# Moving a gate's product with x from TensorE to GpSimd (layer 0) and VectorE (layer 2) in a four-layer graph network

## The chip, the core and the metric

The kernel runs on one core of one Trainium2 chip. The metric is the device time of one execution in microseconds (us). Before the change the median of 14 runs is 3122.3 us (3103.58 to 3138.67).

In the views of the profile PE is TensorE's matmul, PEld its weight load, DVE is VectorE, ACT is ScalarE, POOL is GpSimd and SP is SyncE, which issues most transfers. L1576 is line 1576 of the kernel before. A matmul with float32 operands appears as two PE instructions.

## What is computed

There are 16 graphs (batches) of 1024 nodes with 128 features and a dense 0/1 adjacency of 1024 by 1024 each. Four layers follow each other, each of the form x = layernorm(x + gnn(x, adj)). The two layers that the change touches are attention layers with gates:

```
# layer 0
h = x @ W.T + b;  e = (h @ A) @ h.T;  e = e + e.T
att = softmax(where(adj > 0, e, -9e15), axis=1) * adj
hp  = relu(att @ h)
coeff = sigmoid(concat([x, hp]) @ gate_w.T + gate_b)          # one gate
out = coeff * x + (1 - coeff) * hp
# layer 2: the same attention with zeros for the masked, and three gates
i, f, o = [sigmoid(concat([x, hp]) @ g_w.T + g_b) for g in (ig, fg, og)]
out = o * tanh(sigmoid(i * hp + f * x))
```

So a gate is a dot product of 256 numbers for each node: 128 of them meet x and 128 meet hp. Layer 1 thins the adjacency row by row and runs three neighbourhood averages with batch norms; layer 3 is a graph convolution with two propagations through the normalized adjacency.

## The kernel before

**Layout.** A batch's x lies as s.xn, a tile of 128 partitions by 8 blocks by 128 features: node 128*i + p is in partition p, block i. Its transpose xT is 128 features by 1024 nodes, and TensorE's other operands (hT, G, hpT) have this shape too. A gate's product on TensorE therefore takes block i of xT (128 by 128) as the weights and one (layer 0, L916) or three (layer 2, L1576) columns of the gate's vector as what streams through: one matmul for each block, whose result has one or three columns.

All of this is fast_kernel. A second, general kernel in the same program runs only if flags (`bad` and others) say that the inputs are not of the form that fast_kernel is made for; here it does not run.

**Streams.** Each attention layer has three generators per batch: before (loads, transposes and products up to hT, G and hn), attention (eight tiles jt of scores, mask, softmax and the product with h), and after (gate, residual, norm; in layer 2 all of layer 3 follows in it). in_turn (L793) first runs before alone, for batch 0 in layer 0 and for batches 0 and 1 in layer 2, and then attention of batch b, after of batch b-1 and before of batch b+1 in turns, one yield each. The last batch's after has no attention beside it. In what order an engine then executes is decided by the scheduler of the language's tile layer, which reorders instructions within the engines' queues; each engine then works through its queue strictly in its order, and a wait at its head holds all behind it.

**Layer 0** (us 0 to 765). before (L888) handles eight row blocks `it` of the adjacency: ACT converts a block to bfloat16 with row sums (L897), DVE checks that it holds 0 and 1 only (L900), PE transposes it (L904), DVE writes it as 8-bit floats into the carry tile (L905). Between them stand, at it == 1, the transposes that make xT; at it == 3 hT = W0T xT and the gate's product with x (L914 to L918), which DVE copies into s.gx; at it == 5 G; at it == 7 hn. attention (L930) makes scores on PE (line L723 of a helper), adds the mask and takes the row maximum on DVE (L942), exponentiates on ACT (L946), scales a block of hn (hs, L950) and adds to acc on PE (L953). after (L956) takes relu of acc as hpT (L959), multiplies with the gate's other half (L962), adds s.gx (L964), takes a tanh, and combines: tile r of the pool `work`, one buffer, takes the part of hp (L973) and is added to xn (L974). normed (L772) then takes bn_stats and bn_aggr on DVE, the power -0.5 on POOL (ln_rstd, L744), ln_nb on DVE (L782) and eight scalings on ACT (L784). POOL issues the transfers of x1 (L977) and of the carry tile (L928). All transposes, products and gate results of layer 0 besides scores and acc share two PSUM buffers (ps_h, tag "h").

**Layers 2 and 3** (us 1890 to 3130). before (L1508) finishes layer 1's output, norms it (L1521), makes xT (L1525), hT (L1529), G (L1533) and hn (L1536). s.xT has two buffers and is kept until after. attention (L1539) is as in layer 0 with another mask. after (L1569) takes hpT (L1572), and pg (L1576, L1577): for each of eight blocks a matmul on xT that starts an accumulation and one on hpT that ends it. gt is pg plus the biases (L1579), tanh (L1580) and a scaling (L1581); the combination (L1584 to L1591) and a norm follow. Then layer 3: two elu in a row (L1607 to L1613; in a half of 512 columns, exp on ACT, L1478 or L1474, and two instructions on DVE, L1479/L1480 or L1475/L1476), scaled_parts (L1482: product with a weight, L1489, scaling zn, L1491, and a split into zhi, L1492, and zlo, L1494), propagated (L1497: 32 products with the adjacency, L1503, in two halves), an elu, and both once more; a last norm and the transfer of the result. Transposes and products again share two PSUM buffers (ps_h).

**Weights.** gw (L879 and L1185) holds each gate's vector as two columns of 128, loaded with a strided transfer. row_bcast (L689) loads a row into all partitions; column (L695) loads a vector as one column. `bad` (L675) is a tile of flags that the layer-1 code sets (L1092, L1113) and the last lines sum up (L1647).

Of the kernel before, what the change touches and what calls it, by code (L numbers as in the profile page):

```python
# [9 lines left out]
F32 = mybir.dt.float32  # L10
F16 = mybir.dt.float16
F32R = mybir.dt.float32r
BF16 = mybir.dt.bfloat16
# [4 lines left out]
OP = mybir.AluOpType  # L18
AX = mybir.AxisListType
# [3 lines left out]
P = 128  # L23
# [616 lines left out]
def fast_kernel(ctx: ExitStack, tc: tile.TileContext, t: dict, out: bass.AP, flag: bass.AP):  # L640

    nc = tc.nc
    B, N, D = t["x"].shape
    NT = N // P
# [27 lines left out]
    deg = consts.tile([P, BT], F32, name="deg")  # L672
    dinv = deg

    bad = consts.tile([P, 2, NT, B], F32, name="bad")  # L675
    past = consts.tile([P, NT - 2, B], F32, name="past")
    other = consts.tile([P, BT], F32, name="other")

# [82 lines left out]
    def products(psum, *pairs):  # L761

        for p, c, _ in halves(psum):
            for i, (W, x) in enumerate(pairs):
                nc.tensor.matmul(p, W, x[:, c], start=(i == 0), stop=(i == len(pairs) - 1))  # L765
            yield p, c

    def half_rows(v):

# [97 lines left out]
    with ExitStack() as ph:  # L867
# [8 lines left out]
        work = ph.enter_context(tc.tile_pool(name="l0_work", bufs=1))  # L876
        small = ph.enter_context(tc.tile_pool(name="l0_small", bufs=2))
        b0 = column(wts, t["L0_gnn_W_b"], "l0b")
        gw = wts.tile([P, 2], F32, name="l0gw")  # L879
        with nc.allow_non_contiguous_dma(reason="a vector of 256"):  # L880
            nc.sync.dma_start(gw, t["L0_gnn_gate_w"].rearrange("o (h d) -> d (o h)", d=P))
        gb = row_bcast(wts, t["L0_gnn_gate_b"], 1, "l0gb")
        gbh = wts.tile([P, 1], F32, name="l0gbh")
        nc.vector.tensor_scalar(gbh, gb, 0.5, None, op0=OP.mult)
# [3 lines left out]
        def before(s, b):  # L888

            s.xn = work.tile([P, NT, P], F32, name="xn", bufs=3)  # L890
            nc.sync.dma_start(s.xn, nat(t["x"][b]))
            for it in range(NT):
                c = b * NT + it
                an = work.tile([P, N], F32, name="an", bufs=2)
                nc.sync.dma_start(an, t["adj"][b][it * P:(it + 1) * P, :])
                ab = work.tile([P, N], BF16, name="ab", bufs=2)
                nc.scalar.activation(ab, an, AF.Copy, accum_out=deg[:, c:c + 1])  # L897

                chk = work.tile([P, N], FP8, name="chk")
                nc.vector.scalar_tensor_tensor(chk, an, 0.0, an, op0=OP.is_gt, op1=OP.not_equal,  # L900
                                               accum_out=other[:, c:c + 1], saturate=False)
                pt = ps_h.tile([P, NT, P], BF16, name="pt", tag="h")
                for jt in range(NT):
                    nc.tensor.transpose(pt[:, jt, :], ab[:, jt * P:(jt + 1) * P], identb)  # L904
                nc.vector.tensor_scalar(Y[b][:, :, it * P:(it + 1) * P], pt, 0.0, None, op0=OP.is_gt, saturate=False)  # L905
                if it == 1:
                    xT = work.tile([P, N], F32, name="xT")
                    for p, c, _ in turned(ps_h, s.xn):
                        nc.scalar.copy(xT[:, c], p)
                elif it == 3:  # L910
                    s.hT = work.tile([P, N], F32, name="hT", bufs=2)
                    for p, c in products(ps_h, (W0T, xT)):
                        nc.scalar.activation(s.hT[:, c], p, AF.Identity, bias=b0)
                    pz = ps_h.tile([P, NT], F32, name="pz", tag="h")  # L914
                    for i in range(NT):
                        nc.tensor.matmul(pz[:, i:i + 1], xT[:, i * P:(i + 1) * P], gw[:, 0:1], start=True, stop=True)  # L916
                    s.gx = small.tile([P, NT], F32, name="gx")
                    nc.vector.tensor_copy(s.gx, pz)  # L918
                elif it == 5:
                    s.G = work.tile([P, N], F32, name="G", bufs=2)  # L920
                    for p, c in products(ps_h, (As0, s.hT)):
                        nc.scalar.copy(s.G[:, c], p)
                elif it == 7:
                    s.hn = work.tile([P, N], F32, name="hn")
                    for p, c, _ in turned(ps_h, s.hT):
# [30 lines left out]
        def after(s, b):  # L956

            hpT = work.tile([P, N], F32, name="hpT")
            nc.scalar.activation(hpT, s.acc, AF.Relu)  # L959
            pz = ps_h.tile([P, NT], F32, name="pz", tag="h")  # L960
            for i in range(NT):
                nc.tensor.matmul(pz[:, i:i + 1], hpT[:, i * P:(i + 1) * P], gw[:, 1:2], start=True, stop=True)  # L962
# [205 lines left out]
    class Layers23:  # L1168
# [8 lines left out]
        def weights(self, ps_h):  # L1177
            wts = self.wts
            self.Wl = wts.tile([P, 3, P], F32, name="Wl")
            nc.sync.dma_start(self.Wl, nat(t["L1_gnn_Wl"]))  # L1180
            self.blcol = column(wts, t["L1_gnn_bl"], "blcol")
            self.W2T = transposed(wts, ps_h, matrix(wts, t["L2_gnn_W_w"], "l2W"), "l2WT", "h")
            self.b2 = column(wts, t["L2_gnn_W_b"], "l2b")
            self.As2 = symmetric(wts, ps_h, matrix(wts, t["L2_gnn_A"], "l2A"), "l2As", "h")
            self.gw = wts.tile([P, 2, 3], F32, name="l2gw")  # L1185
            self.gb = wts.tile([P, 3], F32, name="l2gb")
            for i, n in enumerate(("ig", "fg", "og")):
                with nc.allow_non_contiguous_dma(reason="a vector of 256"):
                    nc.sync.dma_start(self.gw[:, :, i], t[f"L2_gnn_{n}_w"].rearrange("o (h d) -> d (o h)", d=P))
                src = t[f"L2_gnn_{n}_b"]  # L1190
# [31 lines left out]
    with ExitStack() as ph:  # L1222
# [187 lines left out]
        for l in range(3):  # L1410
# [9 lines left out]
            for i in range(B + lag[l]):  # L1420
# [32 lines left out]
    with ExitStack() as ph:  # L1453
# [10 lines left out]
        def wide(name, bufs=1, dtype=F32):  # L1464
            return work.tile([P, N], dtype, name=name, bufs=bufs)
# [42 lines left out]
        def before(s, b):  # L1508
# [11 lines left out]
            yield  # L1520
            normed(small, s.xn)  # L1521
            yield
            s.xT = wide("xT", 2)
            for p, c, _ in turned(ps_h, s.xn):
                nc.scalar.copy(s.xT[:, c], p)  # L1525
            yield
            s.hT = wide("hT", 2)
            for p, c in products(ps_h, (W2T, s.xT)):
# [40 lines left out]
        def after(s, b):  # L1569
# [3 lines left out]
            pg = ps_h.tile([P, NT, 3], F32, name="pg", tag="h")  # L1573
            for i in range(NT):
                c = slice(i * P, (i + 1) * P)
                nc.tensor.matmul(pg[:, i, :], s.xT[:, c], gw[:, 0, :], start=True, stop=False)  # L1576
                nc.tensor.matmul(pg[:, i, :], hpT[:, c], gw[:, 1, :], start=False, stop=True)  # L1577
# [106 lines left out]
```

## Time and profile before

| | |
|---|---|
| median of 14 runs | 3122.3 us |
| the profiled execution's own time | 3132.34 us |
| its span, first to last instruction | 3130.6 us |
| mean granted TensorE clock in it | 0.964 |
| gate products with x, layer 0 (L916) | 256 PE instructions, 30.0 us busy, mean 247 ns |
| gate products with hp, layer 0 (L962) | 256 PE instructions, 30.8 us busy, mean 250 ns |
| gate products with x, layer 2 (L1576) | 256 PE instructions, 48.8 us busy, mean 261 ns |
| gate products with hp, layer 2 (L1577) | 256 PE instructions, 51.0 us busy, mean 269 ns |
| copy of gx (L918) on DVE | 16 instructions, 167 ns each |
| ln_rstd on POOL (L744) | 64 instructions, mean 1828 ns |

The busy time of a group counts what its instructions occupy, each from start to end; they overlap in the engine's pipeline, so that the start-to-start distance in the timeline is shorter than the mean. A stretch (a view by windows) lists for a piece of the span the busy time of each engine, the granted TensorE clock (1.00 is full speed), and the share of the transfer engines. A timeline line has the start, the time from the first start to the last end of a run of like instructions, their number (x16), and in brackets how long the engine had been idle before it and who ended that.

### The profile page before, as it was taken

The page shows a single profiled execution, that of the slowest core. Times are in us where ns is not written, and L with a number is a line of the kernel's source. Part 1 is how long each engine was busy: PE and PEld are TensorE (multiplying, and loading weights), DVE is VectorE, ACT ScalarE, POOL GpSimd, SP SyncE. Part 2 cuts the span into 40 slices and gives each one's busy share as a digit, 9 for nine tenths or more (in the row PEclk, how much of TensorE's full clock was granted, in tenths as well). Part 3 has the DMA queues.
Part 4 walks back from the last instruction along what each step waited for, and adds up shares of the span by engine and source line. Part 5 has one row for each costly group of instructions (what it writes and reads, how often), then busy time and mean ns, then how long its engine had stood idle before and what let it go on. Part 6 is the DMA issues. An engine that isn't in the chain of part 4 may idle for free. (4 is left out here: it accounts for less than half of the span.)

```text
span 3130.6 us, 41583 instructions
## 1 busy us (share of the span) xinstructions
PE 2884.0 (92%) x14611; PEld 1782.6 (57%) x14674; DVE 2273.2 (73%) x5875; ACT 2077.5 (66%) x3489; POOL 336.8 (11%) x292
## 2 busy tenths in 40 slices
PE   7999999996899988999999998999999999999996
PEld 4454545453566555777677754555555555555554
DVE  7788888886899984666667665666676666666765
ACT  6777777774678876666666565666666666666663
POOL 0000000003000001111122231001000001110000
PEclk9999999998999999999999998999999999999997
DMA  5344444441000006223366692111111111111000
GB/s 180 113 148 148 134 129 142 140 128 36 1 2 2 2 22 214 81 95 122 123 232 231 219 346 74 41 56 66 54 61 61 55 68 60 54 55 54 21 14 22
DMA packets 123210, 297.68 MB, mean 95 GB/s; under 512 B 13040, under 2 KB 64624, under 8 KB 115824
## 3 DMA queue, kind: packets, MB, share of 16 engines
q1 hardware_dynamic: 102384, 210.93, 21.1%
q0 software_dynamic: 20608, 84.00, 7.2%
q8 instruction: 118, 1.93, 0.3%
q14 instruction: 100, 0.82, 0.1%
HBM read 210.84 MB, written 84.02 MB: 94 GB/s over the span
## 5 line engine op out<-in xcount | busy, mean ns | idle before, releaser
L723 PE MATMUL pmm<-G,hT 128*128 128x512 f32 x1024 | 513.4, 624 | 8.5 <-DVE mx L942 5.2
L723 PEld LDWEIGHTS pmm<-G,hT 128*128 128x128 f32 x1024 | 187.9, 200 | 186.8 <-issue 141.7
L784 ACT ACTIVATE xn<-xn,ln_nb,ln_rstd 128x128 f32<-128x128 f32 x512 | 209.1, 481 | 121.4 <-DVE ln_nb L782 121.2
L1566 PE MATMUL acc<-em,hs 128*128 128x512 f32 x512 | 247.1, 597 | 22.1 <-DVE hs L1563 20.5
L744 POOL TENSOR_TENSOR ln_rstd<-ln_rstd,mhalf 128x8 f32<-128x8 f32 x64 | 117.0, 1828 | 1391.0 <-DVE ln_rstd L741 1077.2
L953 PE MATMUL acc<-em,hs 128*128 128x512 f32 x512 | 253.4, 620 | 13.0 <-DVE hs L950 9.3
L1269 PE MATMUL acc<-a,lo 128*128 128x512 f32 x768 | 238.0, 394 | 2.7 <-DVE lo L1237 2.7
L1269 PE MATMUL acc<-a,hi 128*128 128x512 f32 x768 | 237.9, 394 | 1.7 <-ACT a L1258 1.7
L1130 ACT ACTIVATE q<-s,negc 128x512 f16<-128x512 f32 x256 | 170.2, 693 | 65.8 <-issue 29.3
L1552 DVE CUSTOM_DVE_ANT_0 em<-pmm,msk 128x1024 f32<-128x1024 f32 x128 | 155.9, 1218 | 75.4 <-PE pmm L723 51.5
L1128 PE MATMUL s<-step,carry 128*128 128x384 bf16 (+3 forms) x1035 | 198.6, 302 | 6.8 <-DVE carry L1098 3.2
L1142 ACT ACTIVATE carry<-pc,negone 128x512 fp8e4<-128x512 f32 x256 | 166.4, 693 | 37.9 <-PE pc L1141 27.6
L939 ACT ACTIVATE msk<-carry,l0nbig 128x1024 bf16<-128x1024 fp8e4 x128 | 145.3, 1141 | 66.5 <-DVE mx L942 48.3
L897 ACT ACTIVATE ab<-an 128x1024 bf16<-128x1024 f32 x128 | 134.7, 1052 | 73.1 <-PE pt L904 42.6
L900 DVE SCALAR_TENSOR_TENSOR chk<-an 128x1024 fp8e4<-128x1024 f32 x128 | 156.3, 1221 | 36.6 <-DMA an<-in_adj 36.1
L942 DVE CUSTOM_DVE_ANT_0 em<-pmm,msk 128x1024 f32<-128x1024 f32 x128 | 155.6, 1215 | 27.0 <-PE acc L953 18.8
L1547 ACT ACTIVATE msk<-A,nbig 128x1024 bf16<-128x1024 fp8e4 x128 | 145.4, 1137 | 31.0 <-DVE mx L1552 28.7
L905 DVE TENSOR_SCALAR carry<-pt 128x1024 fp8e4<-128x1024 bf16 x128 | 155.0, 1217 | 14.9 <-PE pt L904 14.8
L1269 PEld LDWEIGHTS acc<-a,lo 128*128 128x128 f32 x768 | 142.8, 188 | 40.3 <-DVE lo L1237 10.2
L953 PEld LDWEIGHTS acc<-em,hs 128*128 128x128 f32 x512 | 93.2, 195 | 125.1 <-issue 95.0
L1566 PEld LDWEIGHTS acc<-em,hs 128*128 128x128 f32 x512 | 92.4, 190 | 117.1 <-issue 79.3
L1269 PEld LDWEIGHTS acc<-a,hi 128*128 128x128 f32 x768 | 141.6, 188 | 30.1 <-ACT a L1258 1.9
(280 smaller groups left out, 6418.8 us busy)
## 6 DMA issues: line engine op xcount, KB each, us to landing
an<-in_adj SPq DMA_DIRECT2D x128, 512.0 KB, 3.7
adj_d<-carry POOLq DMA_DIRECT2D x16, 1024.0 KB, 4.9
A<-dil_d SPq DMA_DIRECT2D x16, 1024.0 KB, 6.3
rdeg<-rdeg_d SPq DMA_DIRECT2D x32, 512.0 KB, 4.4
ag_d<-ag POOLq DMA_DIRECT2D x32, 512.0 KB, 5.3
ag<-ag_d SPq DMA_DIRECT2D x32, 512.0 KB, 6.4
A<-adj_d SPq DMA_DIRECT2D x16, 1024.0 KB, 4.8
xn<-in_x SPq DMA_DIRECT2D x16, 512.0 KB, 4.3
```

What stands on the lines that cost most here:

```text
L723: nc.tensor.matmul(p[:, h * 512:(h + 1) * 512], lhsT, rhs[:, h * 512:(h + 1) * 512], start=True, stop=True)
L784: nc.scalar.activation(r[:, i, :], r[:, i, :], AF.Identity, scale=rstd[:, i:i + 1], bias=nb[:, i:i + 1])
L900: nc.vector.scalar_tensor_tensor(chk, an, 0.0, an, op0=OP.is_gt, op1=OP.not_equal, accum_out=other[:, c:c + 1], saturate=False)
L905: nc.vector.tensor_scalar(Y[b][:, :, it * P:(it + 1) * P], pt, 0.0, None, op0=OP.is_gt, saturate=False)
L942: nc.vector.tensor_tensor_reduce(em, e, msk, 1.0, -3.0e38, op0=OP.add, op1=OP.max, accum_out=mx)
L953: nc.tensor.matmul(s.acc[:, c], hs, em[:, c], start=(jt == 0), stop=(jt == NT - 1))
L1128: nc.tensor.matmul(s[:, lo or 0:], y, twos if lo is None else step[:, :512 - lo], start=(j == 0), stop=(j == len(terms) - 1))
L1130: nc.scalar.activation(q[:, h * 512:(h + 1) * 512], s, AF.Abs, bias=st.negc[:, i:i + 1])
L1142: nc.scalar.activation(Y[b][:, hb, ks], pc, AF.Relu, bias=negone, saturate=False)
L1269: nc.tensor.matmul(acc, part[:, jt, :], pieces[h * NT // 2 + i][:, j, :], start=(jt == 0 and p == 0), stop=(jt == NT - 1 and p == 1))
L1552: nc.vector.tensor_tensor_reduce(em, e, msk, 1.0, 0.0, op0=OP.add, op1=OP.max, accum_out=mx)
L1566: nc.tensor.matmul(s.acc[:, c], hs, em[:, c], start=(jt == 0), stop=(jt == NT - 1))
```

## The change

In layer 0, s.gx no longer comes from TensorE. A new function gate multiplies s.xn with the gate's row (loaded into all partitions as gxr) on GpSimd, 1024 products in a partition, adds halves of the 128 features twice on GpSimd (64 and 32 columns in each block), and sums the remaining 32 on VectorE. It stands at it == 5, after G, and uses tile r of the same pool and name as after's r. In layer 2, 24 VectorE instructions a batch (three gates by eight blocks) multiply a block of s.xn with a gate's row and sum it into a column of s.gx; they stand in before, after xT's copies. after then needs only the product with hpT, and adds s.gx to gt with one more VectorE instruction. xT of layer 2 is no longer kept in s. gw holds only the half for hp. `bad` becomes bfloat16, half its size.

```diff
-    bad = consts.tile([P, 2, NT, B], F32, name="bad")
+    bad = consts.tile([P, 2, NT, B], BF16, name="bad")
...
+    def gate(out, x, g, tmp):
+        nc.gpsimd.tensor_tensor(tmp, x, g[:, None, :].to_broadcast([P, NT, P]), op=OP.mult)
+        for n in (64, 32):
+            nc.gpsimd.tensor_tensor(tmp[:, :, :n], tmp[:, :, :n], tmp[:, :, n:2 * n], op=OP.add)
+        nc.vector.tensor_reduce(out, tmp[:, :, :32], AX.X, OP.add)
...
-        gw = wts.tile([P, 2], F32, name="l0gw")
-            nc.sync.dma_start(gw, t["L0_gnn_gate_w"].rearrange("o (h d) -> d (o h)", d=P))
+        gxr = row_bcast(wts, t["L0_gnn_gate_w"][0, :P], P, "l0gxr")
+        gw = column(wts, t["L0_gnn_gate_w"][0, P:], "l0gw")
...
-                    pz = ps_h.tile([P, NT], F32, name="pz", tag="h")
-                    for i in range(NT):
-                        nc.tensor.matmul(pz[:, i:i + 1], xT[:, i * P:(i + 1) * P], gw[:, 0:1], start=True, stop=True)
-                    s.gx = small.tile([P, NT], F32, name="gx")
-                    nc.vector.tensor_copy(s.gx, pz)
                 elif it == 5:
...
+                    s.gx = small.tile([P, NT], F32, name="gx")
+                    gate(s.gx, s.xn, gxr, work.tile([P, NT, P], F32, name="r"))
...
-            self.gw = wts.tile([P, 2, 3], F32, name="l2gw")
+            self.gxr = []
+            self.gw = wts.tile([P, 3], F32, name="l2gw")
...
+                self.gxr.append(row_bcast(wts, w[0, :P], P, f"l2gxr{i}"))
...
-            s.xT = wide("xT", 2)
+            xT = wide("xT", 2)
...
+            s.gx = small.tile([P, 3, NT], F32, name="gx")
+            for g in range(3):
+                for i in range(NT):
+                    nc.vector.scalar_tensor_tensor(small.tile([P, P], BF16, name="gtmp"), s.xn[:, i, :], 1.0, l2.gxr[g],
+                                                   op0=OP.mult, op1=OP.mult, accum_out=s.gx[:, g, i:i + 1])
...
-                nc.tensor.matmul(pg[:, i, :], s.xT[:, c], gw[:, 0, :], start=True, stop=False)
-                nc.tensor.matmul(pg[:, i, :], hpT[:, c], gw[:, 1, :], start=False, stop=True)
+                nc.tensor.matmul(pg[:, i, :], hpT[:, c], gw, start=True, stop=True)
...
+            nc.vector.tensor_add(gt, gt, s.gx.rearrange("p g t -> p t g"))
```

In the kernel after, the same things have other lines: the function gate is L771 to L774, the 24 VectorE instructions are L1534, the remaining gate products of layer 2 are L1586, and what follows them is ten lines further down than before (acc is L1576, the product with the second-layer weight L1494, the propagation L1508).

More of the change, by code (lines that the diff above doesn't have):

```diff
@@ L878, in fast_kernel @@
         b0 = column(wts, t["L0_gnn_W_b"], "l0b")
-        gw = wts.tile([P, 2], F32, name="l0gw")
-        with nc.allow_non_contiguous_dma(reason="a vector of 256"):
-            nc.sync.dma_start(gw, t["L0_gnn_gate_w"].rearrange("o (h d) -> d (o h)", d=P))
+        gxr = row_bcast(wts, t["L0_gnn_gate_w"][0, :P], P, "l0gxr")
+        gw = column(wts, t["L0_gnn_gate_w"][0, P:], "l0gw")
         gb = row_bcast(wts, t["L0_gnn_gate_b"], 1, "l0gb")
@@ L961, in after @@
             for i in range(NT):
-                nc.tensor.matmul(pz[:, i:i + 1], hpT[:, i * P:(i + 1) * P], gw[:, 1:2], start=True, stop=True)
+                nc.tensor.matmul(pz[:, i:i + 1], hpT[:, i * P:(i + 1) * P], gw, start=True, stop=True)
             co = small.tile([P, NT], F32, name="co")
@@ L1184, in weights @@
             self.As2 = symmetric(wts, ps_h, matrix(wts, t["L2_gnn_A"], "l2A"), "l2As", "h")
-            self.gw = wts.tile([P, 2, 3], F32, name="l2gw")
+            self.gxr = []
+            self.gw = wts.tile([P, 3], F32, name="l2gw")
             self.gb = wts.tile([P, 3], F32, name="l2gb")
             for i, n in enumerate(("ig", "fg", "og")):
-                with nc.allow_non_contiguous_dma(reason="a vector of 256"):
-                    nc.sync.dma_start(self.gw[:, :, i], t[f"L2_gnn_{n}_w"].rearrange("o (h d) -> d (o h)", d=P))
-                src = t[f"L2_gnn_{n}_b"]
+                w, src = t[f"L2_gnn_{n}_w"], t[f"L2_gnn_{n}_b"]
+                self.gxr.append(row_bcast(wts, w[0, :P], P, f"l2gxr{i}"))
+                nc.sync.dma_start(self.gw[:, i:i + 1], bass.AP(tensor=w.tensor, offset=w.offset + P, ap=[[1, P], [1, 1]]))
                 nc.sync.dma_start(self.gb[:, i:i + 1], bass.AP(tensor=src.tensor, offset=src.offset, ap=[[0, P], [1, 1]]))
@@ L1522, in before @@
             yield
-            s.xT = wide("xT", 2)
+            xT = wide("xT", 2)
             for p, c, _ in turned(ps_h, s.xn):
-                nc.scalar.copy(s.xT[:, c], p)
+                nc.scalar.copy(xT[:, c], p)
+            s.gx = small.tile([P, 3, NT], F32, name="gx")
[3 more added lines that the diff above has]
+                                                   op0=OP.mult, op1=OP.mult, accum_out=s.gx[:, g, i:i + 1])
             yield
             s.hT = wide("hT", 2)
-            for p, c in products(ps_h, (W2T, s.xT)):
+            for p, c in products(ps_h, (W2T, xT)):
                 nc.scalar.activation(s.hT[:, c], p, AF.Identity, bias=b2)
```

## The prediction

> **What bounds the kernel now.** I read the engine totals, then the stretches by stage, then the timeline of one batch of layers 2 and 3, engine by engine, with the granted clock beside it.
>
> ```profile
> PE 2884.0 (92%) x14611; PEld 1782.6 (57%) x14674; DVE 2273.2 (73%) x5875; ACT 2077.5 (66%) x3489; POOL 336.8 (11%) x292
> ```
>
> ```profile
> 20.00:765.00 745.00, 693.11 (x3113) 369.72 (x3113) 612.99 (x1469) 545.29 (x887) 70.59 (x48) 0.98 0.41 130
> ...
> 2000.00:2900.00 900.00, 841.13 (x3184) 515.88 (x3183) 609.70 (x1855) 578.89 (x1119) 81.00 (x48) 0.95 0.17 57
> ```
>
> The columns of a stretch are its length and the busy time of PE, PEld, DVE, ACT and POOL. PE is busy 93% of both stages that the edit touches: layer 0 (20 to 765) and layers 2/3 (2000 to 2900). DVE is busy 82% of the first and 68% of the second; POOL has 9% in both. The chain of waits goes back only to 1787 us; there it is mostly PE, with a stretch of DVE, POOL and ACT in each batch.
>
> In layers 2/3 each batch passes the same point, the start of POOL's ln_rstd, every 74.54 us (2062.44 to 2956.88, twelve batches). One batch in the middle took less:
>
> ```profile
> 2212.38:2287.89 75.51, 70.93 (x266) 43.81 (x265) 50.68 (x155) 48.15 (x93) 6.75 (x4) 0.93 0.17 57
> 2287.89:2359.50 71.61, 66.62 (x266) 40.63 (x265) 50.65 (x155) 47.87 (x93) 6.75 (x4) 1.00 0.18 59
> 2359.50:2434.45 74.95, 69.96 (x266) 42.85 (x265) 50.63 (x155) 48.21 (x93) 6.75 (x5) 0.95 0.17 57
> ```
>
> Same instructions, but the granted clock (third column from the end) was 1.00 in the 71.61 us batch and 0.93 to 0.95 in the others. The timeline shows where it falls:
>
> ```profile
> 2406.51 0.28 PE L1576 MATMUL pg<-l2gw,xT 128*128 128x3 f32 x2
> ...
> 2410.69 0.57 PE L1577 MATMUL pg<-l2gw,hpT 128*128 128x3 f32 x2
> 2411.11 1.09 PE L758 MATMUL ph<-identf,hpT 128*128 128x128 f32 x4
> 2412.00 4.53 PE L723 MATMUL pmm<-G,hT 128*128 128x512 f32 x6
> ...
> 2447.34 2.22 PE L1489 MATMUL ph<-U,ehi 128*128 128x128 f32 x16 [2.92 <-DVE ehi L1476]
> ```
>
> The 32 gate instructions (xT and hpT in turn, three columns each) occupy PE from 2406.5 to 2411.1, 0.11 us each until the clock halves at about 2408.9, 0.21 after; the six pmm instructions behind them need 4.53 us, 2.74 in the undisturbed batch. Of the 16 such bursts (3.2 to 4.4 us long) 14 run into a drop; of the 32 of layer 0 (16 instructions, 1.6 to 1.7 us each, but one of 2.3) seven do. The reader should also see PE's 2.92 us wait for elu's result before L1489: that is where DVE is the bound.
>
> **The change part by part.**
>
> *Layer 0, PE.* 128 matmuls on xT go (256 instructions, L916): per batch 16 at 0.106 us, 1.7 us, in all 27 us. PE is the stage's bound, but it already waits 52 of 745 us there, so I take four fifths: −22. Three of the seven drops follow an L916 burst, each 3.4 us at half clock, 1.7 us: −4. DVE's copy of gx (167 ns), for which DVE sat idle 16.9 us, becomes a sum over 256 elements; the nearest row, L1647's reduction of 256 columns, is 385 ns: 16 × 0.22 = 3.5, of which half is on the path: +2. Layer 0: **−24**.
>
> *Layer 0, POOL.* Three instructions a batch (1024, 512 and 256 results in a partition), no row of that kind. Below: an affine select of 128 columns takes 284 ns and a memset of one 93 to 109, so 1.5 ns an element, 1792 elements and three starts, 3.0 us. Above: the pow of 128 columns takes 20749 ns, 162 ns an element, 290 us. I take 3 to 4.5, near the select, since pow is no plain product. In the new order the three stand on POOL ahead of ln_rstd and wait for DVE to release tile r (L974, which starts at 412.66 and is followed on DVE at 413.80); ln_rstd started at 418.72. That leaves 4.9 us: hidden, and costing nothing. The excess over 4.9, if any, holds ln_rstd, then ln_nb in DVE's queue with em and carry behind it, and the x1 transfer. Nothing excludes a slowing of DVE beside POOL either; in that gap DVE does the statistics and L905. The gate's sum on DVE stands behind ln_nb and em, by then POOL is done.
>
> [...]
>
> *Layers 2/3, PE.* 16 of a batch's 32 gate instructions go. In the undisturbed batch they are worth 1.78 us, but not all of it is on the path: behind them stands the em of the next tiles, whose exp on ACT (L1556, 2343.48 there) waits for the norm's eight xn (2340.38), which come from POOL and not from the gates; so hs is ready at 2346.06 as before and the first acc moves from 2347.01 to 2346.1: −0.9. The burst is now like layer 0's, so I expect a drop after one in five (7 of 32), at 1.7 us: +0.3 on the undisturbed 71.61, in place of the 2.9 that the mean batch has over it.
>
> *Layers 2/3, DVE.* 24 products with a sum, 128x128, a batch. Bounds for one: BN_STATS of 128 columns, eight in 1.64 us, follow each other at 0.194; a lone TENSOR_SCALAR of that size is 283 ns, a read of the accumulator 82 (L900), the extra of SCALAR_TENSOR_TENSOR over TENSOR_TENSOR at 512 columns 60 (750 against 691): 0.42. I take 0.25: the 0.194, plus 0.055 that an instruction behind a read of the accumulator starts late (nmx to the next, 0.12 instead of 0.065). In all 6.0 us a batch; DVE has 24 idle, but not where they stand. The new order on DVE is: A's diagonal, then five of them one by one between the eight steps of elu, three between the two zn, four before zlo, twelve between zlo and the sm, rs, hs of four tiles. Walking the 2442 to 2460 stretch with the old durations: the first ehi of the second elu comes 0.6 later (L1489 starts at 2447.96, was 2447.34); zn's second half 0.8 later (2450.44); ACT, which now copies both zhi before xT, gives PSUM back at 2452.3, so L1503 starts there instead of 2450.83; the first hs, 2450.81 before, ends at 2457.0 behind the twelve. PE's new order has 16 L1503 products (3.64 us) ahead of the acc that needs this hs: it arrives at 2456.0 and waits 1.0. The second half and L765 behind it start 2.45 later than before. Nothing later gives this back, PE being the bound again: **+2.45**. Cover that is used up: with 0.20 a product the shift is 1.3, and each 0.01 above 0.25 costs 0.24.
>
> ```profile
> L900 DVE SCALAR_TENSOR_TENSOR chk<-an 128x1024 fp8e4<-128x1024 f32 x128 | 156.3, 1221 | 36.6 <-DMA an<-in_adj 36.1
> ...
> L1480 DVE SCALAR_TENSOR_TENSOR ehi<-prop,c,elo 128x512 f32<-128x512 f32 x32 | 24.0, 751 | 1.1
> L1480 DVE SCALAR_TENSOR_TENSOR ehi<-ph,c,elo 128x512 f32<-128x512 f32 x32 | 23.9, 750 | 1.0
> ...
> L1586 DVE TENSOR_TENSOR x3T<-xn,gt 128x1024 f32<-128x1024 f32 x16 | 19.5, 1216 | 0.0
> ```
>
> These rows carry the full rate: with an accumulator (L900) 1221 ns for 1024, like a plain product (L1586), and two f32 sources in SBUF cost the same as one there and one in PSUM (L1480). [...]
>
> PE's wait before L1489 grows from 2.92 to about 3.6 us. The shorter wait was followed by a drop three times in thirteen; a longer one I give four in five. Much of a drop falls into waits for DVE, so I price it at 1.4: **+1.1**.
>
> Batch: 71.61 − 0.9 + 0.3 + 2.45 + 1.1 = 74.6, against 74.54. What the clock gives, DVE takes: 14 batches, **+1**. In the start (1918 to 1930) DVE is idle 12.5 us, which hides 40 products; the statistics there come a little later: +1. At the end two bursts without an attention beside them lose 1.7 us each, less what the added sum of gt costs: −3. The flag's narrower type, the broadcast loads and the narrower gw loads are a few transfers on SP's queue, in which the steady batches do not wait: 0.
>
> Sum: −24 + 1 + 1 − 3 = **−25**, so 3130.6 becomes 3106 in span, 3132.3 becomes 3107 in time. The profiled execution lies 10 us above the median of 14 (3122.3); from there: **3097**.
>
> **Rivals.** *Slower: the products hold hs.* At 0.42 us each, the upper bound, the batch costs 4.1 us more, 14 × 4.1 = +57: 3154. The sum turns at 0.25 + 25/(14 × 24) = 0.32 us. For it: a lone 128-column row is 0.28, the read-out 0.08. Against: such rows overlap in the timeline. *POOL holds the norm.* If the three take 7 us, ln_rstd comes 2 us late in each batch and DVE, 82% busy, stands: 16 × 1.5 = +24, which cancels the gain: 3121. *The clock pays fully.* If L1489's longer wait costs no drop and a product 0.20, the batch is 71.3, 14 × −3.2 = −45 and in all −71: 3051. *It doesn't do what it says:* layer 0's wait moves from PE to ACT and DVE (ab, carry), half of the −24 is gone: 3109.
>
> **How the numbers follow.** A measurement of this kernel can tell 0.3%, 9.4 us, from no change. Forecast (its own range 3080 to 3113) 0.36; clock pays, in whole or half, 0.18; layer 0 gives half, 0.15 (a third of it above 3113); POOL holds 0.13; products hold 0.18. Faster 0.36 + 0.18 + 0.10 = 0.64; same 0.05 + 0.13 = 0.18; slower 0.18. The range, 3058 to 3142, reaches half way into the outer cases.
>
> **What would show it.** L916 and L1576 gone, L771/L773 on POOL at 3 to 4.5 us a batch in sum and ln_rstd no later than before; layer 0 some 24 us shorter; gate bursts of 1.7 us with the clock mostly at 1.00 behind them; 24 rows of L1534 at a spacing of 0.25; a new PE wait for hs of about 1 us between the halves of the first propagation, and 3.6 us before the second-layer product. The forecast is wrong if L1534's spacing is over 0.32, if POOL's three pass 4.9 us, or if the scheduler's new order in layer 0 makes waits that the old rows don't show.

## The result and the profile after

The change made the kernel slower: the median of 10 runs is 3142.6 us (3134.4 to 3146.0), against 3120.9 us for 47 runs of the kernel before beside it; the ratio is 1.0063, 95% interval [1.0041, 1.0086]. The profiled execution took 3148.2 us, its span is 3146.4, 15.8 more than before.

First the engine totals of after, then its two stages (length; busy time of PE, PEld, DVE, ACT, POOL; clock).

```profile
PE 2832.7 (90%) x14099; PEld 1716.3 (55%) x14162; DVE 2348.1 (75%) x6659; ACT 2079.8 (66%) x3489; POOL 410.2 (13%) x340
```

```profile
20.00:765.00 745.00, 666.27 (x2774) 335.24 (x2775) 618.65 (x1445) 545.82 (x882) 133.65 (x92) 0.99 0.40 131
2000.00:2900.00 900.00, 819.98 (x3008) 486.18 (x3007) 661.37 (x2471) 580.93 (x1125) 82.70 (x49) 0.97 0.17 58
```

PE is busy 51 us less, as meant, and the span has grown all the same. The last ln_rstd of layer 0 tells where: it starts at 776.91 us, before at 761.77, +15.1. From there to the end it is 2369.4 us, before 2368.9. So all of the loss in these two profiles lies in layer 0.

For layer 0 I cut the same piece from each profile: 14 batches, from the start of the first ln_rstd to that of the fifteenth. Before, then after:

```profile
98.61:739.13 640.52, 603.89 (x2654) 320.76 (x2654) 532.79 (x1284) 476.65 (x774) 65.07 (x43) 0.98 0.42 133
```

```profile
102.59:754.15 651.56, 582.76 (x2429) 292.30 (x2428) 542.62 (x1284) 479.30 (x775) 122.21 (x83) 0.99 0.40 130
```

PE's busy time falls by 21.1 us, and its idle time (length less busy) grows from 36.6 to 68.8 us, by 32.2. That leaves +11.0; the other 4 us are the later start (102.59 against 98.61). Some 5 of the 21.1 us are clock and not work: in these pieces the profile grants PE half its clock for 23.9 us before and 13.7 after, and an estimate of what that costs, from the prediction's gate products (0.11 us each at full clock, 0.21 at half), is half of the time. What DVE waited for, in the view of waits over 20 to 765 us (total, times, longest); before, then after:

```profile
DVE chk L900 <- DMA an<-in_adj: 30.8, 27, 2.4
```

```profile
DVE chk L907 <- DMA an<-in_adj: 57.8, 42, 3.1
```

One such wait and what it does, first on DVE, then on PE (both from the timeline of after):

```profile
449.11 1.21 DVE L907 SCALAR_TENSOR_TENSOR chk<-an 128x1024 fp8e4<-128x1024 f32 x1
...
451.58 1.22 DVE L907 SCALAR_TENSOR_TENSOR chk<-an 128x1024 fp8e4<-128x1024 f32 x1
...
456.02 1.23 DVE L907 SCALAR_TENSOR_TENSOR chk<-an 128x1024 fp8e4<-128x1024 f32 x1 [3.15 <-DMA an<-in_adj]
```

```profile
452.90 2.74 PE L723 MATMUL pmm<-G,hT 128*128 128x512 f32 x6
458.52 1.99 PE L723 MATMUL pmm<-G,hT 128*128 128x512 f32 x2 [2.88 <-DVE mx L946]
```

an has two buffers. The load for the third chk here cannot be issued before the first has been read (450.3; SP issues it at 450.69), and it landed at about 455.9, beside the store of the carry tile issued at 449.42. In the new order only an em and one more chk stand between the first and the third, so DVE reaches the third at 452.9, and stands at the head of its queue for 3.15 us. What stands behind it is late too: an rs whose sum ACT has ended at 454.24 runs at 457.17, the em at 457.25; and PE, which needs its score buffer back, waits 2.88. This is the wait of PE that grew most. In the 14 batches (total, times, longest), before, then after:

```profile
PE pmm L723 <- DVE mx L942: 3.3, 7, 0.5
```

```profile
PE pmm L723 <- DVE mx L946: 20.5, 22, 2.9
```

### The profile page after: what moved, and what is told of

It reads as the page before. It is cut to its first block, busy times and chain, and to the rows that moved or that the text cites. A ratio compares the mean times of both kernels' runs of the same rounds, so it can differ in the third digit from the quotient of the medians.

```text
span 3146.4 us, 41425 instructions
## 1 busy us (share of the span) xinstructions
PE 2832.7 (90%) x14099; PEld 1716.3 (55%) x14162; DVE 2348.1 (75%) x6659; ACT 2079.8 (66%) x3489; POOL 410.2 (13%) x340
## 5 line engine op out<-in xcount | busy, mean ns | idle before, releaser
L723 PE MATMUL pmm<-G,hT 128*128 128x512 f32 x1024 | 501.3, 607 | 31.3 <-DVE mx L946 20.7
L723 PEld LDWEIGHTS pmm<-G,hT 128*128 128x128 f32 x1024 | 177.7, 192 | 201.2 <-issue 116.8
L1576 PE MATMUL acc<-em,hs 128*128 128x512 f32 x512 | 248.0, 599 | 25.9 <-DVE hs L1573 24.2
L744 POOL TENSOR_TENSOR ln_rstd<-ln_rstd,mhalf 128x8 f32<-128x8 f32 x64 | 117.1, 1829 | 1093.3 <-DVE nmx L1564 598.8
L950 ACT ACTIVATE em<-em,nmx 128x1024 f32<-128x1024 f32 x128 | 146.2, 1143 | 26.9 <-DVE nmx L948 26.4
L1576 PEld LDWEIGHTS acc<-em,hs 128*128 128x128 f32 x512 | 90.9, 190 | 126.2 <-issue 76.6
```

Source lines behind the costliest of these rows:

```text
L723: nc.tensor.matmul(p[:, h * 512:(h + 1) * 512], lhsT, rhs[:, h * 512:(h + 1) * 512], start=True, stop=True)
L744: nc.gpsimd.tensor_tensor(r, r, mhalf[:, :n], op=OP.pow)
L1576: nc.tensor.matmul(s.acc[:, c], hs, em[:, c], start=(jt == 0), stop=(jt == NT - 1))
```

## The experiments

Below, "14 batches" is the piece just described. "Held" adds up by how much DVE instructions last longer than the median of their own group, where that is over 80 ns. "Half clock" is the time in the 14 batches in which the profile grants PE half its clock; by an estimate from the gate products of the prediction (0.11 us each at full clock, 0.21 at half), work that fills this time would need half of it at full clock. All are microseconds of single profiles.

| kernel | last ln_rstd | 14 batches | PE busy | PE idle | DVE wait before chk | held | half clock |
|---|---|---|---|---|---|---|---|
| before | 761.8 | 640.5 | 603.9 | 36.6 | 27 | 0 | 23.9 |
| after | 776.9 | 651.6 | 582.8 | 68.8 | 55 | 9.0 | 13.7 |
| e1, layer 0 part alone | 768.8 | 643.7 | 577.5 | 66.2 | 52 | 8.9 | 3.4 |
| e3, before, no gx | 744.4 | 625.0 | 579.1 | 45.8 | 32 | 0.3 | 10.2 |
| e4, PE's and GpSimd's | 793.9 | 667.2 | 618.9 | 48.3 | 30 | 7.2 | 34.1 |
| e5, after, hs as product | 746.3 | 623.8 | 574.1 | 49.7 | 38 | 7.8 | 3.4 |
| e6, gate on VectorE | 796.3 | 678.7 | 592.8 | 85.9 | 64 | 0 | 30.7 |
| e7, quarter gate | 770.2 | 649.2 | 586.4 | 62.7 | 56 | 0.3 | 23.9 |
| e9, after, gate at it 3 | 758.9 | 636.7 | 581.3 | 55.4 | 30 | 11.2 | 10.2 |
| e10, after, gate at it 0 | 798.9 | 671.9 | 600.8 | 71.1 | 46 | 13.9 | 68.3 |
| e13, after, room | 776.0 | 656.2 | 588.3 | 67.9 | 14 | 32.5 | 34.1 |
| e14, after, three an | 798.3 | 676.4 | 595.4 | 81.0 | 11 | 37.6 | 61.4 |
| e16, before, three an | 745.1 | 623.7 | 598.3 | 25.5 | 16 | 0 | 10.2 |
| e17, three an, quarter | 734.2 | 617.8 | 578.8 | 39.0 | 15 | 0.3 | 10.2 |
| e18, before, three an, no gx | 726.7 | 607.1 | 574.8 | 32.4 | 14 | 0 | 3.4 |

**The two parts apart (e1, e2).** e1 takes from the diff only the layer 0 part and the narrower flags, e2 only the layer 2 part and the flags.

> Only the layer 0 part (GpSimd's gate, the narrower flags with it), layer 2 as before. If the loss lies in layer 0 as the two profiles say (last ln_rstd of layer 0 at 776.91 against 761.77, +15): some +15 us over before, ratio 1.004 to 1.006, with the periods of 43 and 51 us in turns. If the loss only appears with both parts (shared buffers, another place of the code): within 0.2% of before.

Measured: ratio 1.0036 [1.0012, 1.006], layer 0 at 768.8. Its order is that of after; the 8 us by which it is shorter than there are for the most part clock (3.4 us at half clock in the 14 batches, 13.7 in after).

> Only the layer 2 part (24 VectorE products a batch), layer 0 as before. Theory: the clock pays back what the products cost, 12 batches at 74.21 against 74.54 us, start and end some 5 us worse: 0 to +2 us, ratio 0.999 to 1.001. Rival: the products cost by themselves, and the gain was luck with the clock: +5 us or more.

Measured: 1.0021 [1.0, 1.0042], +6 us. Layer 0 is as before (761.6), and the 12 batches of layers 2/3 take 890.5 us, the same as in after. The narrower flags, which e2 has too, so cost layer 0 nothing. Each part loses, e2 barely (its interval begins at 1), and 0.36 and 0.21% together are about the 0.63% of the change.

**Is it the removal or the addition? (e3, e4)**

```diff
 e3: before, without PE's product
-                        nc.tensor.matmul(pz[:, i:i + 1], xT[:, i * P:(i + 1) * P], gw[:, 0:1], start=True, stop=True)
...
-                    nc.vector.tensor_copy(s.gx, pz)
...
-            nc.vector.tensor_add(co, pz, s.gx)
+            nc.vector.tensor_copy(co, pz)
 e4: before, with GpSimd's gate beside it
+                    gate(small.tile([P, NT], F32, name="gq"), s.xn, gxr, work.tile([P, NT, P], F32, name="r"))
```

> The kernel before without layer 0's gate product with x: TensorE's 16 instructions a batch and VectorE's copy are gone and nothing takes their place (the gate then sees only hp). Theory 1, GpSimd's gate is what costs (VectorE's 128-column scaling is held up to 1 us beside it, tile r is waited for): -24 us, ratio 0.992. Theory 2, TensorE's products were not on the path and the scheduler's new order of VectorE's queue, with chk ahead of its load, is what costs: no gain, 0 to +15 us, and VectorE's wait for adjacency loads up from 27 us towards 53.

> The kernel before, TensorE's product kept and used, with GpSimd's gate added beside it (its result is thrown away), flags narrower. Theory 1 (GpSimd's gate costs what the change loses, 15 us net and 24 us gross): +25 to +40 us. Theory 2 (the order costs, not the gate): within 10 us of before, in either direction, as the scheduler's order falls.

Measured: e3 0.9921 [0.9888, 0.9955], e4 1.011 [1.0076, 1.0144], +32 us. Taking the product off PE is worth 17 us in layer 0 (744.4), and GpSimd's gate costs 32 (793.9 against 761.8). Theory 1 looked right; the next runs showed that this was only half of it. Two reservations belong to these numbers. About 7 of the 17 us are clock (10.2 us at half clock against 23.9), and the rest of e3's gain in the median, 33 us in all, lies in layers 2/3, which the edit does not touch: the profile of e3 has one clock drop in the 12 batches there, before 13. And in e4 PE's busy time is 15.0 us longer than in before at the same work; about 5 of that are clock, the rest is not explained here.

**GpSimd's hold on VectorE, and its length (e5, e6, e7).** In after some hs last 1.27 us and not 0.28; DVE, then POOL beside it:

```profile
423.04 0.28 DVE L785 BATCH_NORM_STATS2 ln_st<-xn 128x6 f32<-128x128 f32 x1
423.23 1.27 DVE L954 TENSOR_SCALAR hs<-hn,rs 128x128 f32<-128x128 f32 x1
424.43 1.44 DVE L785 BATCH_NORM_STATS2 ln_st<-xn 128x6 f32<-128x128 f32 x7
```

```profile
422.07 2.35 POOL L771 TENSOR_TENSOR r<-xn,l0gxr 128x1024 f32<-128x1024 f32 x1 [15.62 <-issue]
424.50 2.07 POOL L773 TENSOR_TENSOR r<-r 128x512 f32<-128x512 f32 x2
427.69 1.65 POOL L744 TENSOR_TENSOR ln_rstd<-ln_rstd,mhalf 128x8 f32<-128x8 f32 x1 [1.11 <-DVE ln_rstd L741]
```

hs ends within 0.1 us of L771, while the statistics run through beside L773.

```diff
 e5: after, hs in layer 0 as a plain product
-                nc.vector.tensor_scalar(hs, s.hn[:, js], rs, None, op0=OP.mult)
+                nc.vector.tensor_tensor(hs, s.hn[:, js], rs.to_broadcast([P, P]), op=OP.mult)
 e6: after, gate on VectorE
-                    gate(s.gx, s.xn, gxr, work.tile([P, NT, P], F32, name="r"))
+                    for i in range(NT):
+                        nc.vector.scalar_tensor_tensor(gtmp, s.xn[:, i, :], 1.0, gxr, op0=OP.mult, op1=OP.mult, accum_out=s.gx[:, i:i + 1])
 e7: after, a quarter of the features on GpSimd, no halves added
+        nc.gpsimd.tensor_tensor(tmp[:, :, :32], x[:, :, :32], g[:, None, :32].to_broadcast([P, NT, 32]), op=OP.mult)
```

> The kernel after, with hs in layer 0 written as a plain VectorE product with the reciprocal broadcast, in place of a scaling with one number a partition; the order of the queues stays nearly the same. In the profile of after eight hs take 1.26 us and not 0.28, each ending when GpSimd's product ends. Theory (this holding is a main part of the loss): no hs over 0.4 us, layer 0 some 8 us shorter, 8 to 10 us less than after in all, about 1.003 over before. Rival (a wait that PE or the loads cover anyway, the order is what costs): as after, 1.006, with the period still 43 and 51 us in turns.

> The kernel after, with layer 0's gate as eight VectorE products with a sum (as layer 2 does it) in place of GpSimd's three instructions and VectorE's sum. It costs VectorE 8 x 0.21 = 1.7 us a batch in place of 0.41 and no GpSimd time. If GpSimd is what costs (it holds VectorE, and VectorE stands before the sum at the start): layer 0 between the kernel without the product (744 us) and before (762), so about -10 us against before in layer 0 and 10 to 25 us less than after. If VectorE's queue is the bound whatever is added to it: as after or worse.

> The kernel after, with only 32 of the 128 features in layer 0's gate product with x: one GpSimd instruction of 256 results a partition in place of three, the same sum on VectorE (the gate misses three quarters of its sum). If GpSimd's length is what costs (4.4 us a batch, with the holding and the late norm): 10 us or more below after, and no hs at 1.26 us. If it is the sum's place in VectorE's queue and the order of the loads: within 5 us of after.

Measured: e5 0.9974 [0.9952, 0.9995], 28 us below after; e6 1.0151 [1.0112, 1.0189]; e7 1.0033 [1.001, 1.0055]. e5 fell far, but not for the reason I gave: the plain product is held too (seven of 128 hs, up to 1.69 us; 7.8 us in sum against 9.0). What the edit changed was the scheduler's order: PE's idle time is 19 us less with the same instructions but this one. e7 keeps after's spacing of the chk, takes the holding away (0.3) and cuts GpSimd to 0.72 us: PE's idle time falls by 6 us only. And e6, without GpSimd's gate, is the worst of these: VectorE's wait before chk is 64 us there. Theory 1 alone falls.

**The order (e9, e10, e11, e12).** The same gate, stated at another `it`; e11 is e9's layer 0 with layer 2 as before, and e12 the kernel before with e5's edit.

```diff
 e9: it == 3 (e10: it == 0)
+                    s.gx = small.tile([P, NT], F32, name="gx")
+                    gate(s.gx, s.xn, gxr, work.tile([P, NT, P], F32, name="r"))
                 elif it == 5:
```

> The kernel after with layer 0's gate stated at it == 3, behind hT, in place of it == 5; the same instructions, GpSimd's order the same. What it moves is the scheduler's order. Measure of an order: VectorE's work between chk of a block and chk two blocks on, which waits for a load into the same buffer; what is missing to 5 us (the load's turn-round in the trace) is added up over blocks 18 to 119. before 38.5 us, after 58.6, e5 38.9, e6 91.3; this kernel 33.2. Theory (the order of chk against the loads sets layer 0's length): last ln_rstd of layer 0 at 740 to 752 us, as e5 (746), in all 3105 to 3118, ratio 0.995 to 0.999. Rival (GpSimd's work and its holding of VectorE set it, e5 was faster for another reason): as after, 770 or more, ratio 1.004 to 1.007.

> The kernel after with layer 0's gate stated at it == 0; the same instructions. The measure of e9 is 71.5 us here, the worst but e6. Theory of the order: layer 0 longer than in after (777), 782 to 792, ratio 1.008 to 1.012. Rival (GpSimd's work sets it): as after or, with the gate further from the norm on GpSimd, shorter: 1.006 or less.

> Only the layer 0 part, stated at it == 3 as in e9; layer 2 as before. Order measure 33.2. Theory: layer 0 as in e9, 740 to 752 us, and 6 us less than e9 for layer 2's part: 3098 to 3110, ratio 0.992 to 0.997, faster than before and than after. Rival: as e1, 1.003 or more.

> A control for e5: the kernel before with hs in layer 0 as a plain product, nothing else. No GpSimd work stands beside it, order measure 36.4 against 38.5. Theory of the order: within 0.2% of before, layer 0 at 756 to 764 us. Rival (the plain product itself is faster, or frees VectorE): 0.5% or more below before.

Measured: e9 1.0026 [1.0002, 1.005], layer 0 at 758.9; e10 1.0134 [1.0097, 1.0171], 798.9; e11 1.0019 [0.9986, 1.0052], 762.1; e12 1.0032 [1.0005, 1.0059], 767.3. So hs as such brings nothing, and the same work (but for hs in e5) in four orders (e5, e9, after, e10) gives layer 0 ends from 746 to 799 us, with the two worst measures at the long end. But e9, with the smaller measure, is 13 us longer than e5, between the two theories; e11 misses its range as well, and e10 is slower than its own. The measure roughly sorts these four, it does not predict them. e10 also ran 68 us of its 14 batches at half clock (after 14, e5 3), so that some 32 of the 53 us between the ends come by way of the clock, whether or not the waits brought the drops about.

**The load in time (e13 to e18).** r lies over hpT and the gate's products over xT; the room gives an a third buffer. e13 is the control with two, e15 has only the layer 0 part, e16 is before with r over hpT and three buffers, e17 is e14 with e7's quarter gate, e18 is e16 with e3's removal.

```diff
-                an = work.tile([P, N], F32, name="an", bufs=2)
+                an = work.tile([P, N], F32, name="an", bufs=3)
-                    gate(s.gx, s.xn, gxr, work.tile([P, NT, P], F32, name="r"))
+                    gate(s.gx, s.xn, gxr, tiles3(xT))
-            r = work.tile([P, NT, P], F32, name="r")
+            r = tiles3(hpT)
```

> A control for e14: the kernel after, with r laid over hpT (whose halves are read before r's are written) and the gate's products laid over xT (read for the last time before), so that the tile r of 4 KB a partition goes; two buffers for an as before. Same instructions. The order measure (see e9) is 20.9 us, the lowest so far. Theory of the order: layer 0's last ln_rstd at 740 to 758 (e5 746, e9 759), ratio 0.995 to 1.002. Rival (GpSimd's work and its holding): 768 or more, 1.005.

> e13 with the room given to a third buffer of an: a load may start one block earlier, so chk no longer waits for the load behind chk two blocks back. Order measure with two buffers 69.0, worse than after; with three 4.1. Theory (the wait of chk for its load is what TensorE's idle time grew by): VectorE's idle before chk in 14 batches from 55 us to under 15, TensorE's idle from 69 to 45 to 52, layer 0 at 735 to 752, although the order itself would be bad with two. Rival (the load is late for another reason, as SP's queue or the bandwidth): chk's wait stays above 30 us and layer 0 at 765 or more.

> Only the layer 0 part with e14's buffers, layer 2 as before. Theory: layer 0 as e14, 735 to 752; layers 2 and 3 as in the kernel before, where 12 batches took 860 to 897 us by the number of clock drops: 3085 to 3112, ratio 0.989 to 0.997. If the third buffer does nothing: 1.003.

> The kernel before (gate on TensorE) with r laid over hpT and three buffers of an. chk's wait (27 us in 14 batches) should go; TensorE is idle 37 us there and is the bound, so half of it at most comes back: layer 0 at 745 to 757 (before 762), ratio 0.994 to 0.999. If e15 is lower than this by 10 us or more, the change's layer 0 part is worth it once the loads are in time; if not, it isn't.

Measured: e13 1.0062 [1.0038, 1.0086]; e14 1.0154 [1.0114, 1.0193], layer 0 at 798; e15 1.0143 [1.0099, 1.0186], 804; e16 0.9902 [0.9867, 0.9936], 745. In the kernel before, the third buffer works: layer 0 gains 17 us (about 7 of them clock, and with r over hpT, which was not run alone there), and e15 is 59 us above that, so the layer 0 part in this form is not worth it. The median of e16 is 41 us below that of before; the rest lies again in layers 2/3, which are untouched and show no clock drop in this profile. Why they drop less is open.

In the changed kernel the theories failed. e13 has the smallest order measure of all (20.9) and little wait before chk (14 us), and its 776 is what the rival forecast. e14 and e15 were to end at 735 to 752; the wait before chk goes there as well (11 us in e14), and layer 0 grows. What has taken its place, in e14, on POOL, on DVE and on PE:

```profile
437.47 3.07 POOL L771 TENSOR_TENSOR xT<-xn,l0gxr 128x1024 f32<-128x1024 f32 x1 [2.81 <-PE ph L765]
440.62 2.93 POOL L773 TENSOR_TENSOR xT<-xT 128x512 f32<-128x512 f32 x2
```

```profile
438.38 3.25 DVE L907 SCALAR_TENSOR_TENSOR chk<-an 128x1024 fp8e4<-128x1024 f32 x1
...
443.58 0.42 DVE L774 TENSOR_REDUCE gx<-xT 128x8 f32<-128x256 f32 x1 [1.95 <-POOL xT L773]
...
445.25 0.29 DVE L954 TENSOR_SCALAR hs<-hn,rs 128x128 f32<-128x128 f32 x1
```

```profile
445.60 6.48 PE L957 MATMUL acc<-em,hs 128*128 128x512 f32 x8 [3.99 <-DVE hs L954]
```

A chk that starts beside L771 takes 3.25 us instead of 1.22, the gate's sum stands at the head of DVE's queue for 1.95 us until POOL is done, and the hs behind it lets PE wait 3.99. Over the acc that follow the clock is halved (6.48 us, eight take 3.60 elsewhere).

> e14 with only 32 of the 128 features in the gate's product with x on GpSimd (one instruction of 256 results a partition; the gate misses three quarters of its sum). In e14 chk's wait for loads was gone (11 us) and yet layer 0 took 798: VectorE was held 38 us beside GpSimd and waited 10 us for its result, in front of hs. Theory now (with the loads on time, GpSimd's gate itself takes the place of that wait): held time near 0, TensorE's idle from 81 to 35 to 50 us, layer 0 at 740 to 760. Rival (some other effect of the new order): 780 or more.

> e16 (before, three buffers of an, 745 us for layer 0) without layer 0's gate product with x, nothing in its place: what the product on TensorE is worth once the loads are on time. Theory: TensorE is idle only 26 of 624 us in e16, so its 25 us of work should come off nearly whole: layer 0 at 718 to 730, ratio 0.980 to 0.988. Rival (VectorE or ScalarE bounds as soon as TensorE has less): 735 or more.

Measured: e17 0.9943 [0.9918, 0.9968], layer 0 at 734; e18 0.9881 [0.9814, 0.9948], 727, so that with the loads in time the product on PE is worth 18 us of layer 0. The whole time does not show it: e18, with 4 runs, is not told apart from e16 (0.9881 and 0.9902), since the 12 batches of layers 2/3, untouched in both, took 880 us in the one profile and 860 in the other. With the loads in time, cutting GpSimd's work from three instructions to a short one takes 64 us off layer 0 (e14 to e17), and with the short gate, the loads in time take 36 off (e7 to e17). Both causes are real, and each hides the other: where one is taken away, VectorE's queue is stopped by the other. The 64 us belong to this placing; laid over xT, the gate waits for PE's last read of it (in e14 GpSimd's idle time before L771 that PE ended is 70.5 us in 16 batches) and so ends late. Some 25 of them, and 7 of the 36, are clock (61.4, 23.9 and 10.2 us at half clock in e14, e7 and e17).

**Layer 2's products alone (e8).** The matmuls on s.xT are left out and nothing replaces them.

> The kernel before without layer 2's products with x on TensorE (16 instructions a batch), nothing in their place (the three gates then see only hp). Theory: these products cost about 0.9 us a batch and let the clock drop, so the period falls from 74.5 to 71 us: 14 x 3.5 = 50 us less, ratio 0.984, and the 24 products that replace them in the change (e2: +6 us) cost all of that. Rival: PE hides them and the clock drops elsewhere instead: less than 15 us.

Measured: 0.9932 [0.991, 0.9954], 20 us less, between the theory's 50 and the rival's 15. e2 against e8, 3128.6 against 3101.0, is 28 us for 24 products in 16 batches, 1.7 us a batch.

## Why the prediction was wrong

**Layer 0, PE: right in the work, wrong in what it is worth.** "PE is the stage's bound ... so I take four fifths: −22": the busy time fell by 21.1 us in 14 batches, about 5 of them clock, for which I had −4. But e3 shows that of 24.8 us of busy time taken off only 15.5 are gained, even with nothing in their place (640.5 to 625.0), and in the change 32.2 us of new idle time take all of it and 11 us more. **This is the step that failed**: the term of −24 for layer 0 prices the removal on the waits of the old order, and layer 0 ended 15.1 us later. The closing sentence named the case, new waits by the scheduler's new order, but the sum gave it no term; the rival "layer 0's wait moves from PE to ACT and DVE" had the direction right and stopped at half of the gain.

**Layer 0, POOL: right in length, wrong in "hidden, and costing nothing".** The three take 4.5 us a batch (2.35 and 2.07), the upper end of 3 to 4.5, and the norm is not late (L744 waits for L741, nine times and 31.8 us in sum from 20 to 780 us, and never for the gate; the wait of ln_nb is 9.2 us in sum, before 12.5). What I had put at nothing, "a slowing of DVE beside POOL", is 9.0 us of holding, and where GpSimd's work is cut with after's chk spacing kept (e7), PE's idle time is 6 us less. The start was not costless either: the first two sums on DVE wait 1.96 and 2.11 us for POOL, and the first ln_rstd comes 4.0 us later.

**How the 32 us of new idle time divide.** By e3 and before, 9 come with the shorter PE work itself. By e5, the gate in a better order adds 4 to that (49.7 against 45.8). The other 19 (68.8 against 49.7) are the order that the scheduler happened to choose, with chk at the head of DVE's queue before its load has landed. The wait that the example above shows is the largest part of it; in e5:

```profile
PE pmm L723 <- DVE mx L946: 7.4, 18, 1.1
```

That is 13.1 us less than in after. These are differences of single profiles, so good to a few us, and they follow from e5's order as a whole; no run changes the place of chk alone. What stays open is why e9 needs 13 us more than e5 with less waiting for loads; clock (10 against 3 us at half clock) and holding (11 against 8) account for a part.

**Layers 2/3: right in the sum, in part by luck.** Mean batch 74.21 us (2079.53 to 2970.03), forecast 74.6. The undisturbed batch of after, and one with a drop:

```profile
2450.27:2523.55 73.28, 66.02 (x250) 38.62 (x249) 54.33 (x204) 47.90 (x93) 6.75 (x4) 1.00 0.17 58
2523.55:2597.90 74.35, 67.46 (x250) 40.18 (x249) 54.41 (x204) 48.01 (x93) 6.75 (x4) 0.98 0.17 57
```

71.61 − 0.9 + 2.45 gave 73.2 for the first. The parts, from PE's timeline and DVE's:

```profile
2463.65 2.31 PE L1494 MATMUL ph<-U,ehi 128*128 128x128 f32 x16 [3.40 <-DVE ehi L1481]
...
2467.99 2.11 PE L1508 MATMUL ph<-A,zhi 128*128 128x512 f32 x8 [0.45 <-ACT xT L1530]
...
2472.09 1.98 PE L1576 MATMUL acc<-em,hs 128*128 128x512 f32 x4 [0.18 <-DVE hs L1573]
...
2499.06 1.84 PE L1586 MATMUL pg<-l2gw,hpT 128*128 128x3 f32 x16
...
2505.82 3.70 PE L723 MATMUL pmm<-G,hT 128*128 128x512 f32 x8 [0.50 <-DVE mx L1558]
2510.10 1.13 PE L765 MATMUL ph<-hb,Wl 128*128 128x512 f32 x2 [0.57 <-DVE yn L1594]
2511.06 1.88 PE L1576 MATMUL acc<-em,hs 128*128 128x512 f32 x4
```

```profile
2468.74 0.28 DVE L1534 SCALAR_TENSOR_TENSOR gtmp<-xn,l2gxr 128x128 bf16<-128x128 f32 x1
2468.95 0.08 DVE L1534 DVE_READ_ACCUMULATOR gtmp<-xn,l2gxr 128x1 f32 x1
2468.95 0.28 DVE L1534 SCALAR_TENSOR_TENSOR gtmp<-xn,l2gxr 128x128 bf16<-128x128 f32 x1
```

The products follow each other at 0.21 us, not 0.25, so the wait for hs is 0.18 and not 1.0; the wait before L1494 is 3.40 (forecast 3.6), and a wait for xT of 0.45 is new. A clock drop follows L1494's wait in 11 batches of 12, where I had given four in five, and none follows a gate burst any more. The clock pays and DVE takes it, as forecast; "the products hold hs" did not come. Against the undisturbed batch of before, two terms missed in opposite directions. DVE's +2.45 came to 1.8 (0.49 up to L1494, 1.31 from there to the product with l2WT), and PE's −0.9 to −0.13 (from the first gate product to the first acc behind it, 12.00 us against 12.13), since the waits of 0.50 and 0.57 above are new there. Start and end, forecast at +1 and −3, came to about +2 (from the last ln_rstd of layer 0 to 2079.53) and +3 (from 2970.03 to the end).

**From the profile to the median: wrong.** I took 10 us off, the distance of the profiled execution from the median. It came from the clock drops in layers 2/3, which the edit changes. In nine profiles with layers 2/3 untouched the 12 batches took 860 to 897 us (mean 876; e12 had no drop, before 13); in ten with the edit 889 to 893. My base was near the slow end, so an edit that came out even on it loses against the median: e2 lost 6 us.

Together: forecast 3107 for the profiled execution, found 3148.2, of which 39 us are layer 0; and its distance from the median is 5.7 us, not 10.

**The best version** is none with the change: before with three buffers for an (e16), ratio 0.9902, with the gate's products on TensorE. The runs that are as fast or faster in layer 0 leave out part of the gate.

## What to carry to other kernels

Before you price work that leaves the busiest engine, look at what the in-order queue beside it waits for: with VectorE busy 82% of layer 0 before, a new order was worth more (53 us between four orders of the same work, some 32 of them by way of the clock) than the work removed (21 us). Where a scheduler writes the order, an edit gives you a new draw of it, so compare several statements of the same edit, and take away the waits that make the order matter (a third buffer) before you judge an edit by one of them. Where one kernel's own executions differ in something that the edit touches (here the clock drops), price the edit on the middle of them, not on the one execution that you have.

## What the hardware showed

Some VectorE instructions that start beside one of GpSimd's products (L771, L773) are held, and others take no longer than elsewhere. In after, all seven hs and all seven ln_rstd scalings (L741) that start beside one end less than 0.1 us behind it (281 ns to as much as 1634, 172 to 426). In e14 all 19 chk that do (1221 to as much as 3261) and all ten hs take longer, and in e5 the plain product for hs took up to 1694 ns, 288 in the median. None of 105 BN_STATS in after is held, nor any of the nine carry and seven em there, which read their large operand from PSUM. GpSimd's product took longer too beside a chk that was already running: of the 16 L771 in after one starts so (at 17.92 us, the chk at 17.76) and took 3259 ns, the others took 2341 to 2367; in e14, where the one at 437.47 us starts beside a chk of 437.11 and took 3.07 us, the median is 3070 ns. What decides which VectorE instructions are held, no run here shows.
